# A new order of the work in a gated state-space layer, with stores issued by GpSimd and other rows for the state

## The chip, the cores and the metric

The kernel runs on one core of a Trainium2 chip. The metric is the device time of one execution in microseconds, the median of several. A core has four computing engines: PE (TensorE, matrix products), DVE (VectorE), ACT (ScalarE) and POOL (GpSimd). SP (SyncE) only issues DMAs here. Every engine takes its own instructions strictly in order and waits on semaphores for the others. The 16 DMA engines of the core carry out what the issuing queues give them.

## The reference

The input is `x`, 8 sequences of 1024 tokens with 512 channels, in float32. Two residual layers follow one another.

The first is an attention layer with 16 heads whose projections are modulated by a condition vector. The change does not touch it.

The second is a gated state-space layer. For every token it computes, cut to what matters:

```
xr, gate = split(x @ W_in.T);  xr += t_emb
xc = silu(causal_conv4(xr) + b_conv)
xn = layernorm(xc)
Bm, Cm, dt = split(xn @ W_xproj.T)          # 16 values each
Ad = 1 - tanh(A_log) * 0.01 * tanh(dt @ W_dt.T + b_dt)
Bd = Bm * min(norm(xn), 1)
h  = clip(h * Ad[:, None] + Bd[:, None] * xn[None, :], -10, 10)     # h: 16 x 1024 per sequence
y  = Cm @ h + D * xn
out = x + (y * silu(gate)) @ W_out.T
```

The recurrence over `h` has 1024 steps, one for each token, and each needs the one before.

## The kernel before

The state of a step has 16 rows for each of 8 sequences, 128 rows in all, one on each SBUF partition, and 1024 columns. The recurrence is rescaled by the running product of the decays, so that a step is one addition with limits on VectorE (`step`, L802): `h = limit(h + xb)`. `xb` is the normalised token `xn`, copied to the 16 rows of its sequence and multiplied by a weight for each row. The copying is done by DMA: `spill` (L622) writes 16 tokens of all sequences (512 KB) from SBUF to DRAM, and `fetch` (L765) reads them back for four steps at a time with 8 broadcasts, one for each sequence, of 256 KB each: 16 rows of 16 KB. `rows(b)` (L514) says which partitions a sequence has: partitions 0 to 63 hold sequences 0 to 3, 64 to 127 hold 4 to 7, and a sequence's 16 rows lie 4 apart. `xb` has three buffers of four steps.

ACT multiplies the weights in (`weigh`, L779), two steps ahead. After four steps `products` (L784) sums the 16 rows of each sequence with the output weights on PE, 16 matrix passes in all. `h` has six buffers, so a step waits until the products of the step six before it are done.

Everything else in the layer is done by chunks of 32 tokens, which are two tiles of 16. For one chunk the work runs like this: `load_x1` reads the layer's input; `conv_mm` (8 blocks) multiplies it by `W_in` on PE; `conv_in` copies it and starts the convolution on ACT; `conv_taps` adds three taps on DVE; `conv_out` applies silu on ACT. `flip_mm` transposes on PE; `stats`, `center`, `deviation` and `scale` make the layer norm on DVE, with a square root on ACT. `spill` follows. `squares` and `lengths` make the norm. `skip` multiplies the tile by `D` in place, so it must wait until the spill has read it. `p_mm`, `p_out`, `p_flip`, `params`, `params_mm` and `params_out` make the 48 parameters of each token; `spread` (L665) sends them to the state's rows with 8 small DMAs (`bca`); `decay` and `weights` make the scan's weights from them. Later `order` and `gate_mm` compute the gate, `add_y` and `gate_y` join it to `y`, `out_flip`, `out_copy` and `out_mm` project it, and `out_store` and `out_send` store it with four DMAs a tile.

The order is written by hand. A plan gives each piece a step (`at(n, f, ...)`), counted from `p0`, one chunk before the chunk's own steps begin; `n0 = p0 + 32` is its first own step. The program is emitted step by step: first `h` of the step, then the pieces planned for it. So three chunks are at work in one stretch of 32 steps, and the plan decides the order of instructions on every engine. A step of the plan is no time: an engine goes on as soon as its semaphores allow. All DMAs of the layer are issued by SP, in the plan's order; each waits for the eighth before it of the same kind of queue, and a broadcast of a new group waits for its `xb` buffer.

Of the kernel before, what the change touches and what calls it, by code (L numbers as in the profile page):

```python
# [15 lines left out]
P = 128  # L16
B = 8
# [6 lines left out]
NS = 16  # L24
TC = 32
TT = 16
EPS = 1e-5
EPS_DM = 1e-8


@with_exitstack
def modulated_attention(ctx, tc, const, x1_d, xu_d, S, x, xT, cond, wT, ident, sT):
# [80 lines left out]
    with tc.tile_pool(name="w0", bufs=2) as wp:  # L113
        s2T = wp.tile([P, 2 * KH, B], F32, name="s2T")
        nc.scalar.activation(s2T, sT, AF.Square)
        for n, name in enumerate(NAMES):
# [5 lines left out]
            for o in range(KH):  # L122
                for k in range(KH):
# [6 lines left out]
                    )  # L130
            nc.vector.tensor_scalar_add(dc[:, n], d_ps, EPS_DM)
        nc.scalar.activation(dc, dc, AF.Sqrt)
# [266 lines left out]
def gated_scan(ctx, tc, const, x1_d, S, w_in, w_conv, cols, ln_g, ln_b, w_x, w_xd, w_dt, b_dt, a_log,  # L399
# [10 lines left out]
    nc = tc.nc  # L410
    NCH = S // TC
    CW = B * TC
    NT = TC // TT
# [18 lines left out]

    def load_chunk(c):
        x1 = two.tile([P, KH, B, TC], F32, name="x1")
        nc.sync.dma_start(
            out=x1.rearrange("p k b t -> p k (b t)"),
            in_=x1_d[c].rearrange("(k p) b t -> p k (b t)", p=P),
        )
        return x1

    win_sb = wp.tile([P, KH, 2 * DI], F32, name="win")
    nc.sync.dma_start(out=win_sb[:, :, 0:DI], in_=w_in[:, 0:DI].rearrange("(k p) o -> p k o", p=P))
    x1_now = load_chunk(0)
    cw = load(w_conv.rearrange("(k p) j -> p k j", p=P), "cw", [P, KI, 4])
    cb = load(cols["b_conv"], "cb", [P, KI])
# [18 lines left out]
    xp = few[0:NS, 0 : 3 * CW].rearrange("p (n b t) -> p n b t", n=3, b=B)  # L464
# [48 lines left out]

    def rows(b):  # L514

        r0 = 64 * (b // 4) + b % 4
        return slice(r0, r0 + 4 * (NS - 1) + 1, 4)

    def by_rows(ap):

# [10 lines left out]
    def at(n, f, *args):  # L531
        plan.setdefault(n, []).append(lambda: f(*args))
# [4 lines left out]
    def load_x1(st, c):  # L537
        st["x1"] = load_chunk(c)
# [82 lines left out]

    def spill(st, i):  # L622
        st["xd", i] = dr.tile([32, 4, DI], F32, tag="xd", name="xd")
        nc.sync.dma_start(out=st["xd", i].rearrange("n r c -> r n c"), in_=st["xt", i])

    def squares(st, i):
        if i == 0:
# [37 lines left out]
    def spread(st):  # L665
        st["bca"] = one.tile([P, 3, TC], F32, name="bca")
        for b in range(B):
            nc.sync.dma_start(out=st["bca"][rows(b)], in_=xp[:, :, b, :])

    def decay(st):  # L670
        bd, cm, ad = (st["bca"][:, n] for n in range(3))
# [83 lines left out]
    def out_send(st, c, i):  # L755
        o_sb = st.pop("o_sb")
        t0 = c * TC + i * TT
        for r in range(4):
            dst = out[:, t0 : t0 + TT, :].rearrange("b (q r) o -> r q b o", r=4)[r]
            nc.sync.dma_start(out=dst, in_=o_sb[32 * r : 32 * r + 32, :])  # L760

    xbs = {}
    hs = {}
# [1 line left out]
    def fetch(g):  # L765

        c, t = divmod(4 * g, TC)
        i, q = divmod(t // 4, TT // 4)
        xb = xbp.tile([P, 4, DI], F32, name="xb")
        for b in (0, 4, 1, 5, 2, 6, 3, 7):  # L770
            src = sts[c]["xd", i].rearrange("(q b) r c -> q b (r c)", q=4)[q, b]
            nc.sync.dma_start(  # L772
                out=xb[rows(b)].rearrange("p r c -> p (r c)"),
                in_=src.unsqueeze(0).to_broadcast([NS, 4 * DI]),
            )
        for r in range(4):
            xbs[4 * g + r] = xb[:, r]
# [35 lines left out]
    for c in range(NCH):  # L813
        st, n0 = sts[c], c * TC
        p0 = n0 - TC
        if c > 0:
            at(p0 - 14, load_x1, st, c)
        at(p0 - 9, begin, st)
        for k in range(KI):
            at(p0 - 8 + 2 * k, conv_mm, st, k)  # L820
            at(p0 - 7 + 2 * k, conv_in, st, k)
            at(p0 - 5 + 2 * k, conv_taps, st, k, (0, 1))
            at(p0 - 4 + 2 * k, conv_taps, st, k, (2,))
            at(p0 - 3 + 2 * k, conv_out, st, k)
        for i in range(NT):
            f0 = p0 + 13 + 4 * i
            at(f0, flip_mm, st, i, 0)
            at(f0, flip_mm, st, i, 1)
            at(f0 + 1, stats, st, i, 0)
            at(f0 + 1, stats, st, i, 1)  # L830
            at(f0 + 1, center, st, i)
            at(f0 + 2, deviation, st, i)
            at(f0 + 3, scale, st, i)
            at(f0 + 4, spill, st, i)
            at(f0 + 4, squares, st, i)
            at(p0 + (20, 26)[i], skip, st, i)
        at(p0 + 14, p_mm, st)
        at(p0 + 16, p_out, st)
        at(p0 + 17, p_flip, st)
        at(p0 + 21, lengths, st)  # L840
        for i in range(NT):
            at(p0 + 22 + i, params, st, i)
            at(p0 + 25 + i, params_mm, st, i)
            at(p0 + 26 + i, params_out, st, i)
        at(p0 + 27, spread, st)
        at(p0 + 30, decay, st)
        at(p0 + 31, weights, st, 0)
        at(n0 + 4, weights, st, 1)

        for i, (xo, gm, gs, ey) in enumerate(  # L850
            ((-2, (1, 5), (3, 7), (21, 22, 25, 28)), (17, (22, 23), (24, 25), (38, 39, 41, 45)))
        ):
            at(n0 + xo, order, st, i)
            at(n0 + ey[0], add_y, st, i)
            at(n0 + ey[1], gate_y, st, i)
            for half in range(2):
                at(n0 + gm[half], gate_mm, st, i, half)
                at(n0 + gs[half], gate, st, i, half)
                at(n0 + ey[2] + half, out_flip, st, i, half)
                at(n0 + ey[2] + 1 + half, out_copy, st, i, half)  # L860
                at(n0 + ey[3] + 2 * half, out_mm, st, i, half)
            at(n0 + ey[3] + 4, out_store, st, i)
            at(n0 + ey[3] + 6, out_send, st, c, i)
    for g in range(S // 4):
        at(4 * g - 9, fetch, g)
        at(4 * g + 4, products, g)
# [13 lines left out]
@with_exitstack  # L880
def network(ctx: ExitStack, tc: tile.TileContext, S, ins, out):
    nc = tc.nc
    const = ctx.enter_context(tc.tile_pool(name="const", bufs=1))
    dram = ctx.enter_context(tc.tile_pool(name="dram", bufs=1, space=DRAM))
    x1_d = dram.tile([S // TC, H, B, TC], F32, name="x1_d")
    xu_d = dram.tile([2, H, S], F32, name="xu_d")
    ident = const.tile([P, P], F32, name="ident")
    nc.sync.dma_start(out=ident, in_=ins["ident"])
    sT = const.tile([P, 2 * KH, B], F32, name="sT")
    nc.sync.dma_start(out=sT, in_=ins["condT"].rearrange("(k p) b -> p k b", p=P))  # L890
    with tc.manual_schedule():
# [74 lines left out]
```

## Time and profile before

| | |
|---|---|
| runs, median (lowest to highest) | 6274.84 us (6273.12 to 6277.6) |
| the profiled execution, its span | 6262.97 us, 6261.2 us |
| PE busy over the span | 93% |
| DVE busy | 72% |
| ACT busy | 61% |
| POOL busy (first layer only) | 20% |
| DMA queue of SP, share of 16 engines | 45.4% |
| first and last `h` start | 3557.8 and 6240.3 us |

A line of the timelines gives the start and the length in microseconds, the engine, the line of the kernel, the operation with its output and inputs, how many instructions were merged, and in brackets the idle time before them with what ended it. A line of waits gives the waiting engine and operation, whom it waited for, the sum in microseconds, the number of times, and the longest. Lines with SPq are DMA issues on SP's queue.

The second layer begins after some 3470 us; the profile's 40 slices show GpSimd idle in all of it.

### The profile page before, as it was taken

How to read it: one execution, taken by the hardware profiler on the slowest of the kernel's cores; microseconds unless marked ns; L12 is line 12 of the kernel's file. 1: busy time of each engine (PE TensorE's matmuls, PEld its weight loads, DVE VectorE, ACT ScalarE, POOL GpSimd, SP SyncE). 2: the span in 40 equal slices, each digit the busy share in tenths (PEclk: the TensorE clock that was granted, in tenths of full speed). 3: DMA queues.
4: the chain of work that ended last, by engine and by line, in shares of the span. 5: the costliest groups of instructions: out<-in, count | busy, mean ns of one | idle time of the engine just before them, and what ended most of it. 6: DMA issues, size and time to landing. Idle time of an engine off the chain costs nothing.

```text
span 6261.2 us, 112973 instructions
## 1 busy us (share of the span) xinstructions
PE 5796.5 (93%) x42960; PEld 3314.5 (53%) x42960; DVE 4484.0 (72%) x6917; ACT 3843.8 (61%) x6743; POOL 1266.2 (20%) x1156
## 2 busy tenths in 40 slices
PE   7999999999999999999999699999999999999998
PEld 5555555655555555555555444444444444444443
DVE  2666666656667666666665488888888888888887
ACT  3555655655556556555554477777777777677675
POOL 2433433434334334343332000000000000000000
PEclk8999999999999999999999899999999999999999
DMA  2112111112121111121211678888888888888787
GB/s 70 35 30 71 30 55 49 35 48 67 30 70 31 55 48 35 48 67 30 55 28 55 177 224 223 221 221 228 225 223 227 222 222 228 220 224 226 221 223 198
DMA packets 396859, 781.65 MB, mean 125 GB/s; under 512 B 196496, under 2 KB 295056, under 8 KB 363552
## 3 DMA queue, kind: packets, MB, share of 16 engines
q1 hardware_dynamic: 396320, 774.44, 45.4%
q8 instruction: 341, 5.59, 0.4%
q14 instruction: 198, 1.62, 0.1%
HBM read 663.62 MB, written 83.89 MB: 119 GB/s over the span
## 4 chain that ended last, share of the span: by engine, by line
PE 60%; DMA 14%; DVE 10%; ACT 8%; SPq 5%; issue 3%; POOL 0%; DVEq 0%; ACTq 0%; POOLq 0%
PE mm_ps L153 16%; PE t_ps L262 13%; PE s_ps L252 9%; DMA xb<-xd 8%; PE mm_ps L269 8%; DVE h L806 5%; DMA xd<-xt 4%; PE o_ps L745 4%; SPq L772 4%; PE in_ps L547 4%; ACT pr L370 3%; PE y_ps L793 3%; ACT pT L367 1%; PE g_ps L705 1%; PE in_ps L551 1%
## 5 line engine op out<-in xcount | busy, mean ns | idle before, releaser
L360 DVE TENSOR_REDUCE nmax<-s_ps 128x1 f32<-128x1024 f32 x1024 | 1206.2, 1220 | 478.0 <-PE s_ps L255 477.4
L806 DVE CUSTOM_DVE_ANT_0 h<-h,xb,lim 128x1024 f32<-128x1024 f32 x1024 | 1374.7, 1342 | 209.7 <-PE y_ps L793 71.7
L367 ACT COPY pT<-t_ps 128x512 f32<-128x512 f32 x1024 | 549.8, 589 | 1378.8 <-PE t_ps L262 1378.5
L262 PEld LDWEIGHTS t_ps<-ident,pr 128*128 128x128 f32 x8192 | 909.7, 141 | 646.4 <-issue 453.2
L782 ACT ACTIVATE xb<-xb,ws 128x1024 f32<-128x1024 f32 x1024 | 1135.9, 1145 | 62.4 <-DVE ws L682 31.3
L370 ACT ACTIVATE pr<-s_ps,nmax 128x1024 f32<-128x1024 f32 x1024 | 1139.6, 1127 | 6.1 <-DVE nmax L360 5.7
L262 PE MATMUL t_ps<-ident,pr 128*128 128x128 f32 x8192 | 1096.1, 277 | 30.7 <-ACT pT L367 28.5
L793 PE MATMUL y_ps<-h,yw 128*32 128x512 f32 x4096 | 675.5, 617 | 159.7 <-DVE h L806 159.6
L252 PE MATMUL s_ps<-kT,qT 32*128 32x512 f32 x2048 | 601.1, 641 | 4.4 <-ACT pr L370 4.4
L389 POOL TENSOR_SCALAR pr<-pr,rinv 128x1024 f32<-128x1024 f32 x512 | 572.6, 1118 | 145.6 <-DVE rinv L388 142.9
L255 PE MATMUL s_ps<-k,q 32*128 32x512 f32 x2048 | 578.2, 640 | 0.0
L269 PEld LDWEIGHTS mm_ps<-pT,vt 128*32 128x32 f32 x16384 | 438.0, 110 | 235.1 <-issue 94.3
L705 PE MATMUL g_ps<-win,x1t 128*128 128x512 f32 x1024 | 508.5, 643 | 58.1 <-ACT sq_ps L631 51.3
L269 PE MATMUL mm_ps<-pT,vt 128*32 128x128 f32 x16384 | 517.6, 274 | 47.5 <-ACT vt L200 18.5
L547 PE MATMUL in_ps<-x,win 128*128 128x256 f32 x2048 | 490.9, 383 | 28.9 <-ACT xt L733 17.4
L375 POOL TENSOR_SCALAR pr<-pr,rinv 128x1024 f32<-128x1024 f32 x256 | 286.5, 1119 | 1109.5 <-PE t_ps L262 741.0
L547 PEld LDWEIGHTS in_ps<-x,win 128*128 128x128 f32 x2048 | 389.8, 192 | 152.4 <-issue 71.6
L384 POOL TENSOR_SCALAR pr<-pr,rinv 128x1024 f32<-128x1024 f32 x256 | 286.3, 1118 | 882.6 <-DVE rinv L383 855.8
L745 PE MATMUL o_ps<-wout,xt 128*128 128x512 f32 x1024 | 463.7, 596 | 0.7 <-ACT xt L733 0.7
L793 PEld LDWEIGHTS y_ps<-h,yw 128*32 128x32 f32 x4096 | 133.9, 110 | 545.6 <-DVE h L806 295.0
L381 DVE COPY pT<-t_ps 128x512 f32<-128x512 f32 x512 | 352.2, 688 | 77.2 <-PE t_ps L262 76.8
L705 PEld LDWEIGHTS g_ps<-win,x1t 128*128 128x128 f32 x1024 | 198.2, 204 | 384.6 <-issue 229.5
(129 smaller groups left out, 6750.7 us busy)
## 6 DMA issues: line engine op xcount, KB each, us to landing
xb<-xd SPq DMA_DIRECT2D x2048, 256.0 KB
xd<-xt SPq DMA_DIRECT2D x64, 512.0 KB
xq<-in_x SPq DMA_DIRECT2D x16, 1024.0 KB
q<-qT SPq DMA_DIRECT2D x128, 128.0 KB
xr<-in_xT SPq DMA_DIRECT2D x64, 256.0 KB
xu_d<-xr SPq DMA_DIRECT2D x64, 256.0 KB
xr<-xu_d SPq DMA_DIRECT2D x64, 256.0 KB
x_d<-xr SPq DMA_DIRECT2D x64, 256.0 KB
```

The source lines that it names most:

```text
L153: nc.tensor.matmul(ps, w, x, start=(k == 0), stop=(k == KH - 1))
L252: nc.tensor.matmul(s_ps[i][:, 0:HW], st["q"][r, qc], st["k"][r, 0:HW], start=True, stop=True)
L262: nc.tensor.transpose(ps[:, j], pr[:, c0 : c0 + P], ident)
L269: nc.tensor.matmul(av[r], vt[:, kt, r], pT[:, i, kt], start=(kt == 0), stop=(kt == KT - 1), skip_group_check=True,)
L360: nc.vector.tensor_reduce(nmax[i], s_ps[i], AX.X, ALU.max, negate=True)
L370: nc.scalar.activation(fresh[i], s_ps[i], AF.Exp, bias=nmax[i], accum_out=rsum[i])
L547: nc.tensor.matmul(ps, win_sb[:, kk, k * P : (k + 1) * P], st["x1"][:, kk].rearrange("p b t -> p (b t)"), start=(kk == 0), stop=False,)
L705: nc.tensor.matmul(ps, st["xo", i][:, k], win_sb[:, k, DI + half * 512 : DI + (half + 1) * 512], start=(k == 0), stop=(k == KH - 1),)
L745: nc.tensor.matmul(ps, st["gT", i][:, k, :], wout_sb[:, k, :], start=False, stop=(k == KI - 1), skip_group_check=True,)
L782: nc.scalar.mul(xbs[n], xbs[n], sts[c]["ws"][:, t : t + 1])
L793: nc.tensor.matmul(st["y", i][32 * r : 32 * r + 32, hf * 512 : (hf + 1) * 512], yws[i][:, 4 * q + r, :], hs[4 * g + r][:, hf * 512 : (hf + ...
L806: nc.vector._custom_dve(dve_ops.TENSOR_ADD_SAT, out=h, in0=last["h"], in1=xbs.pop(n), s0=lim[:, 0, t : t + 1], s1=lim[:, 1, t : t + 1],)
```

## The change

Three things change. First, the plan: nearly every piece of a chunk gets another step. Second, `load_chunk`, `spill`, `spread` and `out_send` issue their DMAs from GpSimd; the broadcasts of `fetch` stay on SP. Third, a sequence's rows: sequences 0 to 3 have rows 32 to 95, 4 apart, so each has 8 rows in either half of the partitions; 4 and 5 have rows 0 to 31, 6 and 7 rows 96 to 127, 2 apart. The order of the eight broadcasts changes with it, and the host builds its small tables (`mask_y`, `b_dt`, `a_log`) by the same map. What is computed, and the number of instructions that compute it, stay.

```diff
+def state_rows(b):
+    if b < B // 2:
+        return 32 + b, 4
+    return 96 * (b // 6) + b % 2, 2
...
     def load_chunk(c):
         x1 = two.tile([P, KH, B, TC], F32, name="x1")
-        nc.sync.dma_start(
+        nc.gpsimd.dma_start(
...
     def rows(b):
-        r0 = 64 * (b // 4) + b % 4
-        return slice(r0, r0 + 4 * (NS - 1) + 1, 4)
+        r0, d = state_rows(b)
+        return slice(r0, r0 + d * (NS - 1) + 1, d)
...
     def spill(st, i):
-        nc.sync.dma_start(out=st["xd", i].rearrange("n r c -> r n c"), in_=st["xt", i])
+        nc.gpsimd.dma_start(out=st["xd", i].rearrange("n r c -> r n c"), in_=st["xt", i])
...
     def spread(st):
         for b in range(B):
-            nc.sync.dma_start(out=st["bca"][rows(b)], in_=xp[:, :, b, :])
+            nc.gpsimd.dma_start(out=st["bca"][rows(b)], in_=xp[:, :, b, :])
...
     def out_send(st, c, i):
-            nc.sync.dma_start(out=dst, in_=o_sb[32 * r : 32 * r + 32, :])
+            nc.gpsimd.dma_start(out=dst, in_=o_sb[32 * r : 32 * r + 32, :])
...
-        for b in (0, 4, 1, 5, 2, 6, 3, 7):
+        for b in (4, 6, 0, 1, 5, 7, 2, 3):
```

The plan's steps, counted from `p0`; where two are given they are for the two tiles, and with a stroke for the two halves of a tile:

```
                before                            after
load_x1         -14                               -11
begin           -9                                -14
conv_mm k       -8+2k                             -9+2k
conv_in k       -7+2k                             -8+2k
conv_taps k     -5+2k, -4+2k                      -7+2k, -6+2k
conv_out k      -3+2k                             -5+2k
flip_mm         13, 17                            10, 13
stats, center   14, 18                            11, 15
deviation       15, 19                            12, 16
scale           16, 20                            14, 17
spill           17, 21                            15, 21
squares         17, 21                            17, 19
skip            20, 26                            30, 22
p_mm, p_out, p_flip   14, 16, 17                  16, 19, 20
lengths         21                                19
params          22, 23                            21, 20
params_mm       25, 26                            22, 21
params_out      26, 27                            24, 24
spread, decay   27, 30                            26, 30
weights         31, 36                            35, 34
order           30, 49                            36, 49
gate_mm         33/37, 54/55                      39/42, 50/53
gate            35/39, 56/57                      41/43, 52/58
add_y, gate_y   53 54, 70 71                      53 56, 65 67
out_flip        57/58, 73/74                      58/58, 71/72
out_copy        58/59, 74/75                      60/65, 75/75
out_mm          60/62, 77/79                      61/67, 77/78
out_store       64, 81                            68, 81
out_send        66, 83                            73, 83
```

`fetch`, `products` and `weigh` keep their steps: 9 before a group's first step, 4 after it, and 2 before each step.

More of the change, by code (lines that the diff above doesn't have):

```diff
@@ L816, in gated_scan @@
         if c > 0:
-            at(p0 - 14, load_x1, st, c)
-        at(p0 - 9, begin, st)
+            at(p0 + -11, load_x1, st, c)
+        at(p0 + -14, begin, st)
         for k in range(KI):
[L820 to L845, printed above, removed]
-        at(p0 + 30, decay, st)
[L847 to L863, printed above, removed]
+            at(p0 + -9 + 2 * k, conv_mm, st, k)
@@ new lines, in gated_scan @@
+            at(p0 + -8 + 2 * k, conv_in, st, k)
+            at(p0 + -7 + 2 * k, conv_taps, st, k, (0, 1))
+            at(p0 + -6 + 2 * k, conv_taps, st, k, (2,))
+            at(p0 + -5 + 2 * k, conv_out, st, k)
+        at(p0 + 10, flip_mm, st, 0, 0)
+        at(p0 + 10, flip_mm, st, 0, 1)
+        at(p0 + 11, stats, st, 0, 0)
+        at(p0 + 11, stats, st, 0, 1)
+        at(p0 + 11, center, st, 0)
+        at(p0 + 12, deviation, st, 0)
+        at(p0 + 14, scale, st, 0)
+        at(p0 + 15, spill, st, 0)
@@ new lines, in gated_scan @@
+        at(p0 + 17, squares, st, 0)
+        at(p0 + 30, skip, st, 0)
+        at(p0 + 13, flip_mm, st, 1, 0)
+        at(p0 + 13, flip_mm, st, 1, 1)
+        at(p0 + 15, stats, st, 1, 0)
+        at(p0 + 15, stats, st, 1, 1)
+        at(p0 + 15, center, st, 1)
+        at(p0 + 16, deviation, st, 1)
+        at(p0 + 17, scale, st, 1)
+        at(p0 + 21, spill, st, 1)
+        at(p0 + 19, squares, st, 1)
+        at(p0 + 22, skip, st, 1)
+        at(p0 + 16, p_mm, st)
+        at(p0 + 19, p_out, st)
@@ new lines, in gated_scan @@
+        at(p0 + 20, p_flip, st)
+        at(p0 + 19, lengths, st)
+        at(p0 + 21, params, st, 0)
+        at(p0 + 22, params_mm, st, 0)
+        at(p0 + 24, params_out, st, 0)
+        at(p0 + 20, params, st, 1)
+        at(p0 + 21, params_mm, st, 1)
+        at(p0 + 24, params_out, st, 1)
+        at(p0 + 26, spread, st)
+        at(p0 + 30, decay, st)
+        at(p0 + 35, weights, st, 0)
+        at(p0 + 34, weights, st, 1)
+        at(p0 + 36, order, st, 0)
+        at(p0 + 39, gate_mm, st, 0, 0)
@@ new lines, in gated_scan @@
+        at(p0 + 41, gate, st, 0, 0)
+        at(p0 + 42, gate_mm, st, 0, 1)
+        at(p0 + 43, gate, st, 0, 1)
+        at(p0 + 53, add_y, st, 0)
+        at(p0 + 56, gate_y, st, 0)
+        at(p0 + 58, out_flip, st, 0, 0)
+        at(p0 + 60, out_copy, st, 0, 0)
+        at(p0 + 61, out_mm, st, 0, 0)
+        at(p0 + 58, out_flip, st, 0, 1)
+        at(p0 + 65, out_copy, st, 0, 1)
+        at(p0 + 67, out_mm, st, 0, 1)
+        at(p0 + 68, out_store, st, 0)
+        at(p0 + 73, out_send, st, c, 0)
@@ new lines, in gated_scan @@
+        at(p0 + 49, order, st, 1)
+        at(p0 + 50, gate_mm, st, 1, 0)
+        at(p0 + 52, gate, st, 1, 0)
+        at(p0 + 53, gate_mm, st, 1, 1)
+        at(p0 + 58, gate, st, 1, 1)
+        at(p0 + 65, add_y, st, 1)
+        at(p0 + 67, gate_y, st, 1)
+        at(p0 + 71, out_flip, st, 1, 0)
+        at(p0 + 75, out_copy, st, 1, 0)
+        at(p0 + 77, out_mm, st, 1, 0)
+        at(p0 + 72, out_flip, st, 1, 1)
+        at(p0 + 75, out_copy, st, 1, 1)
+        at(p0 + 78, out_mm, st, 1, 1)
@@ L864, in gated_scan @@
+        at(p0 + 81, out_store, st, 1)
+        at(p0 + 83, out_send, st, c, 1)
     for g in range(S // 4):
@@ L913, in cols @@
         return np.asarray(v).reshape(-1, P).T
-    mask_y = np.broadcast_to(
-        np.eye(B, dtype=np.float32).reshape(2, 1, 4, B), (2, NS, 4, B)
-    ).reshape(P, B)
+    batch_of, state_of = np.zeros(P, int), np.zeros(P, int)
+    for b in range(B):
+        r0, d = state_rows(b)
+        batch_of[r0 + d * np.arange(NS)] = b
+        state_of[r0 + d * np.arange(NS)] = np.arange(NS)
+    mask_y = np.eye(B, dtype=np.float32)[batch_of]
     cond_k = np.zeros((P, P), np.float32)
@@ L923, in rows @@
     def rows(v):
-        return np.tile(np.repeat(np.asarray(v), 4), 2)[:, None]
+        return np.asarray(v)[state_of][:, None]
     arrays = {
```

## The prediction

> **What bounds the kernel now.** I read the table by stage first, then the waits and timelines of one chunk, then the scan's last chunk. The second layer is a recurrence of 1024 steps, 32 to a chunk. In the timeline of VectorE, step `h` runs from 3557.8 to 6241.6 us, so the layer's steady part is 2683.8 us, 31.65 chunks of 84.8 us. The table by stage (columns PE, weight loads, DVE, ACT, POOL busy; PE clock; DMA share; GB/s):
>
> ```profile
> 4700.00:5100.00 400.00, 364.31 (x1614) 190.71 (x1614) 335.36 (x483) 285.33 (x492) 0.00 (x0) 0.98 0.81 224
> ```
>
> PE looks 91% busy, DVE 84%, DMA 81%, ACT 71%. Nobody is full; GpSimd does nothing. The PE figure flatters: the products `y_ps` stand busy while they wait for `h`. Timeline of TensorE in one chunk:
>
> ```profile
> 4614.96 1.38 PE L793 MATMUL y_ps<-h,yw 128*32 128x512 f32 x6
> 4619.45 3.14 PE L793 MATMUL y_ps<-h,yw 128*32 128x512 f32 x10 [3.10 <-DVE h L806]
> ...
> 4647.67 1.92 PE L793 MATMUL y_ps<-h,yw 128*32 128x512 f32 x16
> 4649.52 3.70 PE L745 MATMUL o_ps<-wout,xt 128*128 128x512 f32 x8
> 4653.06 1.89 PE L547 MATMUL in_ps<-x,win 128*128 128x256 f32 x8
> 4654.79 0.60 PE L551 MATMUL in_ps<-ident,cond 128*128 128x256 f32 x2
> 4655.22 1.89 PE L547 MATMUL in_ps<-x,win 128*128 128x256 f32 x8
> ```
>
> Undisturbed (start to start) one group's products take 1.85, half an output projection 3.54, one convolution block 2.16. With such prices PE has 70 us of work in 84.8. The waits of 4300 to 5500 us (14.15 chunks) say who stops whom:
>
> ```profile
> PE y_ps L793 <- DVE h L806: 67.7, 42, 3.1
> DVE xt L637 <- DMA xd<-xt: 58.8, 28, 4.1
> DVE h L806 <- PE y_ps L793: 36.6, 15, 3.7
> DVE stat L597 <- PE x_ps L592: 32.8, 14, 2.4
> ```
>
> PE waits for DVE and DVE for PE in the same chunk: `h` has six buffers, so products and steps can part by about one group of four steps. A group with much PE work stops DVE, the next with much DVE work stops PE. On top, DVE waits 4.2 us a chunk in `skip` for the spill to land. That is the bound: an uneven plan, not a full engine.
>
> The DMA is close behind. First the start of the layer, where little else moves. Timeline of VectorE:
>
> ```profile
> 3533.03 1.22 DVE L637 TENSOR_TENSOR xt<-xt,d_bc 128x1024 f32<-128x1024 f32 x1 [7.09 <-DMA xd<-xt]
> ```
>
> The spill that it waited for, on the SP queue:
>
> ```profile
> 3522.58 0.65 SPq L624 DMA_DIRECT2D xd<-xt  x1
> ```
>
> The chain of waits in the last chunk:
>
> ```profile
> 6198.04 6.98 DMA xb<-xd
> 6205.02 0.02 issue
> 6205.03 7.35 DMA xb<-xd
> 6212.38 0.02 issue
> 6212.40 7.02 DMA xb<-xd
> ```
>
> A spill of 512 KB takes 10.4 us with no broadcast in flight. Eight broadcasts (2.1 MB) take about 7.3 us when DMA alone paces the steps: 0.91 us each, 18 GB/s on each of 16 engines.
>
> [...] Against their being the bound now: DVE waits for broadcasts only some 2 us a chunk, and SP waits 129 us in these 14 chunks for DVE to free a slot.
>
> [...]
>
> **The change, part by part.** No arithmetic is added. 19 of 83 DMA issues per chunk (2 spills, 8 output stores, 8 `bca`, 1 `x1`) leave SP for GpSimd; 64 broadcasts stay.
>
> (1) Plan. I lay each line's price on its step, before and after, and add per group of four steps. Prices (us): PE products 1.87, gate half 3.54, output half 3.44 (+0.9 residual in the first), convolution block 2.16, `p_mm` 3.46, flips 0.3 to 0.5. DVE `h` 1.26, tap 0.47, stats 0.65, center 1.57, scale 1.20, skip, add and gate 1.15, params 0.80, decay 1.48, weights 0.41, deviation 0.42. ACT weigh 1.05, conv_in 0.73, conv_out 0.67, order 1.28, squares 1.25, params_out 0.70, gate, copies and store 0.5. A group lasts as long as its fullest engine:
>
> Before: PE 9.7, 9.7, 2.9, 14.0, 3.1, 9.0, 8.0, 14.0; DVE 7.9, 10.6, 6.9, 8.3, 9.5, 11.6, 7.1, 9.8; ACT at most 9.0 (group 7). Maxima 9.7+10.6+6.9+14.0+9.5+11.6+9.0+14.0 = 85.3.
>
> After: PE 9.6, 8.1, 6.8, 10.6, 8.9, 8.7, 7.2, 10.5; DVE 11.0, 7.9, 8.4, 9.5, 7.0, 8.9, 8.5, 10.5; ACT 8.8 and 9.3 in groups 2 and 5. Maxima 11.0+8.8+8.4+10.6+9.3+8.9+8.5+10.5 = 76.0.
>
> Totals are the same in both (PE 70.3, DVE 71.7, ACT 57.4). DVE's 71.7 of 84.8 is the 84% of the table by stage. The sum of maxima for before lies 0.5 us from the measured 84.8: what it leaves out (spill waits, slots) is about what the slack across groups gives back. I take 76.0 for after, with less to smooth and less to wait for.
>
> (2) Spill and skip. First tile: skip moves from 3 steps after the spill to 15; its share of the 4.2 us goes. Second tile: the plan puts skip one step after the spill, but GpSimd can issue it once scale (5 steps before skip) and the older output store ahead of it are done. From scale DVE has five `h`, lengths, two params and add_y, 9.4 us, before skip. At today's 10.4 us plus 1 to 2 us of queue, DVE stops 2 to 3 us; spread over 16 engines, none. I take 1.0 on top of 76.0: 77.0 us per chunk, range 74 to 80.
>
> (3) SP queue. The 19 issues at about 0.6 us leave it; also the wait for every eighth DMA before, which after a spill held the broadcasts. SP then holds 64 x 0.63 = 40 us of issues in 77. It was not the bound: nothing by itself, cover for DMA.
>
> (4) `bca` from GpSimd. It is issued after params_out (step 24), wanted by decay (step 30): six steps of 2.4 us, 14.4. The trace shows no GpSimd DMA. From below I bound an issue by SP's 0.63 us[...]. At 1 us[...] eight issues and 2 us of landing take 10: hidden. At 2 us: 18, so 3.6 us a chunk late; ACT stops in tanh, behind it weigh and then `h`.
>
> (5) Row map. Broadcasts need 64 x 0.91 = 58 us a chunk; with stores spread evenly (128 KB per engine, 7 us) 65, below 77. Worth nothing on the path if so[...].
>
> (6) Ends. At the start the first skip no longer holds the second tile's scale (7.1 us idle at 3533), nor a spill the `bca` issues: -8. The last store from GpSimd: +2.
>
> Sum on the profiled execution (6262.97, span 6261.2): -7.8 x 31.65 = -247, -8, +2 = -253, 6010; the median of the runs is 12 higher: 6022.
>
> **Rivals.** DMA becomes the bound: GpSimd's stores still sit on four engines together[...]. Then 1440 KB at 18 GB/s is about 82 us a chunk: -2.8 x 31.65 = -89, with the ends 6180[...]
>
> Floor: slack across groups swallows the rest and DVE alone counts, 71.7 plus 1 us of gaps between back-to-back `h` (0.17 each): 72.7, -383, 5890. Against: single waits between engines stay.
>
> Slower: the `bca` issues are slow. Six steps cover eight issues up to (14.4 - 2)/8 = 1.55 us; the 7.8 us gained are gone at 2.5 us each. At 3 us they come 24 + 2 - 14.4 = 11.6 us late, 3.8 more than gained: +120 and the ends, 6390.[...]
>
> That the row map does nothing visible is part of the first case.
>
> **How the numbers follow.** Even plan, 74 to 80 us a chunk (5930 to 6120): 0.60. DMA-bound, 6120 to 6260: 0.18. Floor, below 5930: 0.07. Slower: 0.12. Within 0.2% (12 us, about what a measurement of this kernel can tell): 0.03. Range 5925 to 6235 leaves out the slower case, most of the floor and a little of the DMA case.
>
> **What would show it.** Right: a chunk of about 77 us, DVE near 93%, no long `y_ps` wait for `h` and no stats wait over 1 us, the first tile's skip without a wait, first `h` near 3550. DMA rival: `h` or ACT's weigh wait for `xb`, SP never waits for DVE. Slower: ACT waits for `bca` in the tanh of decay (L672 before the change). My number is wrong if single waits inside a group, which the sum of maxima cannot see, grow past what slack gives back.

## The result, and the profile after

| | before | after |
|---|---|---|
| runs, median (lowest to highest) | 6276.22 us (6273.12 to 6281.06) | 6315.93 us (6313.14 to 6327.47) |
| ratio, with its 95% interval | | 1.0072 [1.006, 1.0083] |
| span of the profiled execution | 6261.2 us | 6325.4 us |
| first and last `h` start | 3557.8 and 6240.3 us | 3562.3 and 6298.7 us |
| end of the span after the last `h` start | 20.9 us | 26.7 us |

The change makes the kernel 0.7% slower. The forecast was 6022 us and faster; 6316 lies outside its range too. The profiled executions lie 64.2 us apart, the medians 39.7, so the profiled one of after is a little above its median. Of the 64.2, 4.5 us lie ahead of the first `h`, 53.9 in the recurrence and 5.8 behind it. A chunk should have become 77.0 us long; it became 86.5 on average (2736.4 us over 31.65 chunks).

The table by stage of the kernel after. The columns are as before: length of the stage, then PE, weight loads, DVE, ACT and POOL busy, TensorE's granted clock, DMA share, GB/s. The first line is one steady stretch, the others are parts of one chunk.

```profile
4700.00:5100.00 400.00, 335.46 (x1577) 183.75 (x1575) 328.67 (x466) 281.04 (x483) 54.34 (x94) 0.92 0.82 222
...
4630.00:4652.00 22.00, 22.00 (x95) 11.07 (x94) 20.95 (x29) 17.50 (x30) 4.52 (x7) 1.00 0.88 227
4653.00:4667.00 14.00, 0.76 (x7) 0.52 (x5) 7.07 (x6) 3.60 (x8) 3.57 (x7) 0.64 0.98 232
4667.00:4690.00 23.00, 21.55 (x100) 13.83 (x101) 14.40 (x24) 11.69 (x21) 0.51 (x1) 0.85 0.61 163
```

The mean over 400 us (DVE 82%, DMA 82%) looks like the kernel before. The parts do not. For 22 us of a chunk PE is always busy and DVE nearly so, which is what an even plan should look like. Then, for 14 us, PE does nothing and DVE is busy half of the time, while the DMA engines are busy 98% of the time. And in the 23 us after that PE runs at 0.85 of its clock. The waits of 4300 to 5500 us (14 chunks) of the kernel after name the two places:

```profile
PE in_ps L554 <- DMA x<-x_d: 184.5, 14, 14.7
DVE xt L644 <- DMA xd<-xt: 139.0, 14, 11.9
ACT xb L789 <- DMA xb<-xd: 79.2, 24, 7.4
ACT rs L621 <- DVE mv L609: 49.3, 14, 4.2
DVE xc L574 <- ACT xc L567: 40.1, 26, 6.9
```

PE waits 13.2 us a chunk for `x1` (the DMA `x<-x_d`), once each time. DVE waits 9.9 us a chunk in `skip` for the spill, and 2.9 for the convolution that stands behind PE's wait. The three waits that bound the kernel before are no longer among the long ones: in the whole layer `y_ps` waits only 15.9 us for `h`, where it was 67.7 in 14 chunks. So the plan did even out the work, and two landings took the place of what it removed.

One chunk on TensorE, kernel after (timeline):

```profile
4652.94 0.82 PE L663 MATMUL xp_ps<-ident,pt 128*128 128x128 f32 x6
4668.45 3.75 PE L554 MATMUL in_ps<-x,win 128*128 128x256 f32 x8 [14.69 <-DMA x<-x_d]
4671.99 1.06 PE L558 MATMUL in_ps<-ident,cond 128*128 128x256 f32 x2
4672.98 2.45 PE L800 MATMUL y_ps<-h,yw 128*32 128x512 f32 x16
4675.36 1.99 PE L554 MATMUL in_ps<-x,win 128*128 128x256 f32 x8
```

And what GpSimd issued for it, from its timeline:

```profile
4636.14 0.69 POOL L631 DMA_DIRECT2D xd<-xt  x1 [21.09 <-DVE xt L627]
4640.68 2.35 POOL L767 DMA_DIRECT2D out<-o_sb  x4 [3.85 <-ACT o_sb L759]
4644.32 0.69 POOL L631 DMA_DIRECT2D xd<-xt  x1 [1.29 <-DVE xt L627]
4645.00 0.80 POOL L442 DMA_DIRECT2D x<-x_d  x1
4662.39 3.57 POOL L675 DMA_DIRECT2D bca<-few  x7 [16.59 <-ACT few L668]
```

The two spills, four output stores and `x1` are issued within 10 us of each other: the two spills 8.2 us apart, `x1` 0.7 us after the second. In the kernel before the spills are 15.4 us apart. There SP issued them and `x1`:

```profile
4613.90 0.57 SPq L624 DMA_DIRECT2D xd<-xt  x1
4614.59 0.40 SPq L435 DMA_DIRECT2D x<-x_d  x1
...
4629.30 0.57 SPq L624 DMA_DIRECT2D xd<-xt  x1
```

They landed 10.5 and 11.3 us later, by the end of `skip`'s waits (kernel before, VectorE):

```profile
4624.37 1.22 DVE L637 TENSOR_TENSOR xt<-xt,d_bc 128x1024 f32<-128x1024 f32 x1 [3.12 <-DMA xd<-xt]
...
4640.62 1.23 DVE L637 TENSOR_TENSOR xt<-xt,d_bc 128x1024 f32<-128x1024 f32 x1 [1.39 <-DMA xd<-xt]
```

In the kernel after `skip` of the second tile waits longer (VectorE):

```profile
4660.66 1.23 DVE L644 TENSOR_TENSOR xt<-xt,d_bc 128x1024 f32<-128x1024 f32 x1 [6.71 <-DMA xd<-xt]
```

The second spill lands at 4660.66, 16.3 us after its issue, and `x1` at 4668.45, 23.4 us after its own. For the spill this chunk is a mild one: from 4300 to 5500 us the second spill of a chunk lands 20.0 us after its issue, the first 14.5 (medians). DVE stopped from 4653.95 on, PE from 4653.76 on. The convolution block that comes first after PE's idle time takes 3.75 us, the next 1.99. The granted clock is at 0.50 from 4657.03 to 4674.10, that is also for the first 5.65 us of PE's work, and at 1.00 from there to 4690.

### The profile page after: what moved, and what is told of

Read it like the earlier page. It is cut to its first block, busy times and chain, and to the rows that moved or that the text cites. A ratio compares the mean times of both kernels' runs of the same rounds, so it can differ in the third digit from the quotient of the medians.

```text
span 6325.4 us, 113455 instructions
## 1 busy us (share of the span) xinstructions
PE 5664.1 (90%) x42960; PEld 3322.2 (53%) x42960; DVE 4474.7 (71%) x6917; ACT 3837.2 (61%) x6743; POOL 1617.6 (26%) x1764
## 5 line engine op out<-in xcount | busy, mean ns | idle before, releaser
L554 PE MATMUL in_ps<-x,win 128*128 128x256 f32 x2048 | 551.9, 417 | 411.9 <-DMA x<-x_d 411.9
L554 PEld LDWEIGHTS in_ps<-x,win 128*128 128x128 f32 x2048 | 411.8, 208 | 578.9 <-issue 460.9
L800 PE MATMUL y_ps<-h,yw 128*32 128x512 f32 x4096 | 515.3, 611 | 23.6 <-DVE h L813 15.9
L712 PE MATMUL g_ps<-win,x1t 128*128 128x512 f32 x1024 | 470.9, 603 | 2.5 <-ACT x1t L707 2.5
L574 DVE SCALAR_TENSOR_TENSOR xc<-xr,cw,xc 128x256 f32<-128x256 f32 x768 | 369.2, 481 | 111.9 <-ACT xc L567 98.6
L767 POOL DMA_DIRECT2D out<-o_sb x256 | 151.2, 597 | 1148.7 <-ACT o_sb L759 1144.4
L388 DVE COPY pT<-t_ps 128x512 f32<-128x512 f32 x512 | 351.7, 687 | 79.2 <-PE t_ps L269 78.8
```

The source lines that it names most:

```text
L554: nc.tensor.matmul(ps, win_sb[:, kk, k * P : (k + 1) * P], st["x1"][:, kk].rearrange("p b t -> p (b t)"), start=(kk == 0), stop=False,)
L800: nc.tensor.matmul(st["y", i][32 * r : 32 * r + 32, hf * 512 : (hf + 1) * 512], yws[i][:, 4 * q + r, :], hs[4 * g + r][:, hf * 512 : (hf + ...
```

## The experiments

Ratios are to the kernel before on the same chip. What an expectation calls one part "alone" is that part put into the kernel before; all else is the kernel after with the edit shown.

### Which part costs?

**rows_only**: the row map and the order of the broadcasts, on the kernel before.

```diff
-        for b in (0, 4, 1, 5, 2, 6, 3, 7):
+        for b in (4, 6, 0, 1, 5, 7, 2, 3):
...
+        r0, d = state_rows(b)
+        return slice(r0, r0 + d * (NS - 1) + 1, d)
```

> The kernel before with the new state rows and the new order of broadcasts alone. Theory A (GpSimd's large transfers land late because they take turns with the broadcasts; the plan is good): broadcasts get about 13% slower, as the last chunk of the changed kernel shows (8.3 us for eight against 7.4 before), but stay hidden behind the steps: 6270 to 6300, with the loss in the last chunk, where DMA alone paces the steps (+6 us). Theory C (the rows make DMA the bound): a chunk of 84.8 becomes 89 us, 6380 to 6420. If the rows help as the prediction had it, the last chunk's groups take under 7.3 us.

**pool_only**: the four `nc.sync` that became `nc.gpsimd` (`x1`, spill, `bca`, output), on the kernel before.

```diff
-        nc.sync.dma_start(out=st["xd", i].rearrange("n r c -> r n c"), in_=st["xt", i])
+        nc.gpsimd.dma_start(out=st["xd", i].rearrange("n r c -> r n c"), in_=st["xt", i])
```

> The kernel before with its four kinds of small DMA and stores issued by GpSimd alone, old plan, old rows. Theory A: x1 lands some 21 us after its issue where the plan gives 16, and each spill 16 us where the plan gives 8, so PE and DVE stop for 5 and about 2 x 6 us a chunk more than now's 4.2: 6450 to 6700. Theory B (the new plan is too tight, whoever issues): no change, 6250 to 6300.

**plan_only**: the new steps alone; all DMAs on SP, rows as before.

```diff
-            at(p0 - 14, load_x1, st, c)
+            at(p0 + -11, load_x1, st, c)
...
-            at(p0 - 8 + 2 * k, conv_mm, st, k)
+            at(p0 + -9 + 2 * k, conv_mm, st, k)
```

> The kernel before with the new plan alone, all DMAs on SP, old rows. Theory A: the balance of the groups shows; x1 and the second spill are held up behind the broadcasts on SP, but land in 8 to 11 us: 6030 to 6280, a chunk of 77 to 84 us. Theory B: 6290 or more, PE waiting for x1 10 us or more a chunk here too.

**x1_sp**: the kernel after, with `x1` loaded from SP again.

```diff
-        nc.gpsimd.dma_start(
+        nc.sync.dma_start(
             out=x1.rearrange("p k b t -> p k (b t)"),
```

> The changed kernel with the load of x1 alone back on SP. Theory A: PE's wait for x1 falls from 13.2 us a chunk to 5 to 8, the wait for the second spill stays at about 10: 6316 less 31 x 5 to 8, 6070 to 6160. Theory B: the load issued two steps before its use stays late: 6290 or more.

| | median us | ratio |
|---|---|---|
| rows_only | 6285.63 | 1.0031 [1.0016, 1.0045] |
| pool_only | 6370.04 | 1.0157 [1.0142, 1.0172] |
| plan_only | 6361.68 | 1.0145 [1.013, 1.0161] |
| x1_sp | 6326.76 | 1.009 [1.0075, 1.0105] |

Each part alone makes the kernel slower, and the three together cost less than the plan alone or GpSimd alone. With the plan alone, the waits are those of the kernel after (kernel plan_only, waits of 4300 to 5500 us):

```profile
PE in_ps L547 <- DMA x<-x_d: 205.8, 14, 15.6
DVE xt L637 <- DMA xd<-xt: 182.0, 14, 13.8
```

So the two stops come with the plan, on either queue. On SP the reason is in part another: in one chunk the second spill leaves at 4662.06, 10.9 us after `scale`, behind broadcasts and stores, and lands 12.2 us later. GpSimd alone keeps the old waits between products and steps and gets new ones for `bca` (kernel pool_only, same view):

```profile
PE y_ps L793 <- DVE h L806: 75.6, 58, 3.1
DVE xt L637 <- DMA xd<-xt: 68.8, 14, 7.9
ACT bca L672 <- DMA bca<-few: 49.8, 13, 4.8
...
DVE bca L673 <- ACT bca L672: 39.7, 14, 3.8
```

With `x1` on SP it lands 8.6 us after its issue in place of 21.2 (medians), but it is issued later, behind a group's broadcasts, and PE waits as long as before: 191.3 us in 14 chunks. Moving `x1` alone to the other queue mends nothing.

### Is it the wait in skip, or the shape of x1's load?

Two thoughts were tried here: that `x1` lands late because it is cut into rows of 1 KB, and that DVE's stop in `skip` is the loss, so that a later `skip` would mend it.

**packed**: `x1` laid out in DRAM so that its load reads rows of 4 KB.

```diff
-    x1_d = dram.tile([S // TC, H, B, TC], F32, name="x1_d")
+    x1_d = dram.tile([S // TC, P, KH, B, TC], F32, name="x1_d")
```

> The changed kernel with x1 kept in DRAM in the order of the partitions, so that a row of the load is 4 KB instead of four times 1 KB; nothing else. Theory A (each packet from GpSimd's queue waits for a broadcast's packet, so the count of packets sets the landing): x1 lands in 8 to 11 us instead of 21, PE's wait for it falls from 13 us a chunk to 0 to 3; the wait for the second spill (10 us) stays and then sets the chunk at 80 to 85: 6080 to 6210. Theory D (the bytes set the landing, or the load waits behind the spill on its queue): it still lands in 17 to 21 us, 6290 to 6330.

**skip_late**: `skip` of the second tile seven steps later.

```diff
-        at(p0 + 22, skip, st, 1)
+        at(p0 + 29, skip, st, 1)
```

> The changed kernel with skip of the second tile seven steps later (29 instead of 22). The two waits lie beside each other in time: while DVE waits for the spill, PE waits for x1. So theory A expects DVE's wait for the spill to go and the time to stay within 6280 to 6320, since x1 alone still stops PE, and through h's buffers DVE. If the spill is the one that decides: 6050 to 6150.

**packed_late**: both.

> Both edits, the packed x1 and the later skip. Theory A: both waits go and the sum of the groups' maxima comes out, 76 to 78 us a chunk: 5950 to 6040. Theory E (with the waits gone the DMA is the next bound): 80 to 84 us a chunk, ACT waiting for broadcasts more than 3 us a chunk: 6080 to 6200.

**packed_late_oldrows**: both, with the rows and the order of the broadcasts of the kernel before.

> Both edits and the old rows with the old order of the broadcasts. If the new rows cost broadcasts: 10 to 60 us faster than the one with both edits and new rows. If they help, as the prediction had it: slower by 10 to 100 us. If the steps cover the broadcasts either way: within 10 us.

| | median us | ratio |
|---|---|---|
| packed | 6314.33 | 1.0073 [1.0056, 1.009] |
| skip_late | 6476.02 | 1.0329 [1.0314, 1.0344] |
| packed_late | 6475.36 | 1.0326 [1.031, 1.0341] |
| packed_late_oldrows | 6362.85 | 1.0148 [1.0133, 1.0163] |

The first thought fell: with rows of 4 KB `x1` lands 21.7 us after its issue and nothing moves. The second fell harder. With `skip` out of the way the kernel lost another 160 us (kernel skip_late, waits of 4300 to 5500 us):

```profile
PE in_ps L554 <- DMA x<-x_d: 229.2, 13, 21.4
DVE xc L574 <- ACT xc L567: 189.8, 13, 19.8
```

I read the stop in `skip` as a relief for the DMA engines: while DVE stands, no `xb` buffer comes free, and SP must hold the next broadcasts back; without it they go on. That is not shown by itself: SP waits 378.6 us for `h` in this stretch of skip_late, as it does in the kernel after (380.2). What is shown is that `x1` lands 25.7 us after its issue in place of 21.2 (medians) and PE waits 17.6 us a chunk. The second spills land no later as a rule (19.5 us against 20.0, medians), though some do: one issued at 4708.16 lets the `bca` issue that waits for it go at 4736.11, 28.0 us later. So the stop in `skip` was not the loss. What was left to try was the time that the spill spends on the DMA engines.

### The spill, in one piece or in four

The destination of a spill begins with a dimension of 4, the four quarters of a token's rows in DRAM. That it runs on 4 engines for this reason was the author's assumption; no run had shown it. The theory, called F where a letter is used: these 512 KB on few engines, beside broadcasts that keep the engines busy (16 of their packets are under way at once for 636 of the 1200 us from 4300 to 5500 us of the kernel before), are what lands late, and `x1` stands behind them on the same engines. The same bytes as four DMAs, one for each quarter, each begin with a dimension of 32 on both sides. If F holds, they spread and land sooner.

**split**: the kernel after with the spill cut in four. **before_split** is the same cut in the kernel before, on SP.

```diff
-        nc.gpsimd.dma_start(out=st["xd", i].rearrange("n r c -> r n c"), in_=st["xt", i])
+        for r in range(4):
+            nc.gpsimd.dma_start(out=st["xd", i][:, r], in_=st["xt", i][32 * r : 32 * r + 32])
```

> The changed kernel with each spill cut into four DMAs of 32 partitions by 1024, so that the slowest dimension of both sides is 32 instead of 128 and 4[...]. The packed load left x1's landing at 21.7 us, so the count of packets is not the reason. Theory F (the spill runs on four engines, which are full; the load of x1 stands behind it on them): the spill lands in 5 to 8 us instead of 16, x1 in 6 to 10, both waits go: 5970 to 6060, a chunk of 76 to 79 us. Theory G (a transfer from GpSimd gets a small share of every engine while broadcasts are in flight, however it is cut): the spill still takes over 12 us, x1 over 17: 6250 to 6330.

> The kernel before with each spill cut into four DMAs. Theory F: DVE's wait for the spill (4.2 us a chunk, 130 us in all) goes, part of it taken up by other waits: 6140 to 6230; the spill lands in about 5 us. If the landing does not depend on the shape: 6265 to 6300, a little slower for six more issues a chunk.

**split_late** has the cut and `skip` at 29; **split_late_oldrows** is that on the old rows.

> The same with skip of the second tile at 29. Theory F: the spill is in time already, so within 20 us of the one before. Theory G: 6400 to 6480, as with the uncut spill.

> The same again with the old rows and the old order of broadcasts. With the uncut spill the new rows cost 113 us. If they cost broadcasts on all engines and broadcasts set the pace again: 40 to 120 us faster than with the new rows. If with the spill cut the steps cover the broadcasts: within 20 us.

| | median us | ratio |
|---|---|---|
| split | 6099.32 | 0.9724 [0.971, 0.9739] |
| before_split | 6166.4 | 0.9829 [0.9815, 0.9844] |
| split_late | 6119.8 | 0.9762 [0.9747, 0.9776] |
| split_late_oldrows | 6114.99 | 0.9746 [0.973, 0.9762] |

One line of the program is worth 217 us in the kernel after and 105 in the kernel before. The landings of 4300 to 5500 us of the kernel after (columns: DMA, queue and operation, number, size, median us from issue to landing):

```profile
xd<-xt POOLq DMA_DIRECT2D x27, 512.0 KB, 16.3
...
x<-x_d POOLq DMA_DIRECT2D x13, 512.0 KB, 21.2
```

The same view of split:

```profile
xd<-xt POOLq DMA_DIRECT2D x123, 128.0 KB, 4.9
...
x<-x_d POOLq DMA_DIRECT2D x15, 512.0 KB, 10.8
```

A piece of the spill lands in 4.9 us (the four are issued within 2.0 us) in place of 16.3 for the whole, and `x1`, which was not touched, in half its time. Late `skip` now costs 20 us where it had cost 160.

The traces also keep a record of every packet that the DMA engines moved, with its queue, size, start and length. It shows four at a time. In pool_only the last spill, issued at 6243.3, has GpSimd's queue to itself: of its 128 packets of 4 KB four are under way for 5.9 us, five for 0.3, and otherwise fewer. In split the four pieces issued at 4627.31 have 14 packets or more under way for 1.5 us. From GpSimd the four are not always the same: in x1_sp its queue carries only spills, output stores and the small `bca`, and from 4300 to 5500 us seven to twelve packets of 4 KB are under way for 25 us. On SP, in the kernel before, the packets of spills and output stores together are mostly four at a time and hardly ever more than five.

The record shows too who stands behind whom. In the kernel before, `x1` comes in 512 packets of 1 KB. Of the load that SP issued at 4614.59, right behind a spill, 384 packets had ended 5.8 us later; the other 128, a quarter, ended from 8.5 to 10.6 us after the issue, and the spill's last packet in between, at 9.3. All 31 loads behind a spill show such a gap behind the 384th packet, of 1.7 to 3.7 us. In before_split the gap is gone, and the 512 packets are over 4.9 us after the issue (median) in place of 10.8. I read this as a spill on four of the sixteen engines, with `x1` behind it on these four and only there; the record does not name the engines. What it shows is that on SP's queue a quarter of `x1` ends with the spill and the rest does not. From GpSimd the packets of both have 4 KB and can't be told apart; that `x1` stands behind the spill there too is read from the landings (21.2 us behind whole spills, 10.8 behind cut ones).

What is left in split (waits of 4300 to 5500 us, 15 chunks):

```profile
PE in_ps L554 <- DMA x<-x_d: 96.6, 15, 9.1
DVE xc L574 <- ACT xc L567: 87.7, 30, 7.8
...
DVE xt L645 <- DMA xd<-xt: 4.7, 1, 4.7
```

The wait in `skip` is gone (one in 15 chunks), but PE still stops 6.4 us a chunk for `x1`. That is the part of the change that the prediction's sum does not contain at all: `load_x1` moved from 6 steps ahead of the first `conv_mm` to 2.

### What the plan and GpSimd earn once the spill is cut

**plan_split** and **pool_split** are plan_only and pool_only with the cut spill.

> The kernel before with the new plan and each spill cut in four; all DMAs stay on SP, old rows, x1 at 11 steps before p0. Theory A (the plan earns the gain, GpSimd only serves it by keeping spill and x1 out of SP's queue of broadcasts): x1 is issued late behind a group's broadcasts, TensorE waits 8 to 14 us a chunk for it, 6150 to 6250 us. Theory B (with the spill cut the queue does not matter): 6090 to 6120 us, as the changed kernel with the cut spill.

> The kernel before with its four kinds of DMAs issued by GpSimd and each spill cut in four; old plan, old rows. Theory A (the plan earns the gain): about the kernel before with the cut spill, 6150 to 6190 us, with the waits between products and steps as there. Theory B (leaving SP earns part of it): 6100 to 6140 us. If bca stays late as with the queues alone and an uncut spill, 6200 us or more.

| spill cut in four | DMAs on SP | on GpSimd |
|---|---|---|
| old plan | 6166.4, 0.9829 [0.9815, 0.9844] (before_split) | 6175.15, 0.9846 [0.9831, 0.986] (pool_split) |
| new plan | 6159.33, 0.9817 [0.9801, 0.9834] (plan_split) | 6099.32, 0.9724 [0.971, 0.9739] (split, new rows) |

Neither earns anything alone; the intervals of the first three overlap. With the new plan on SP the landings are late (kernel plan_split, same waits):

```profile
PE in_ps L547 <- DMA x<-x_d: 123.3, 15, 9.0
DVE xt L638 <- DMA xd<-xt: 99.2, 15, 7.3
```

and with GpSimd under the old plan the uneven groups are still there (kernel pool_split, same waits):

```profile
PE y_ps L794 <- DVE h L807: 74.4, 49, 3.1
...
DVE h L807 <- PE y_ps L794: 45.3, 15, 3.6
DVE stat L597 <- PE x_ps L592: 35.1, 15, 2.4
```

The plan removes the waits between the engines and asks for prompt landings; a queue of its own makes the landings prompt. On this evidence each is worth something only with the other, 60 to 76 us together. How much of that the rows give is not separated, since of the four kernels split alone has the new ones. But split_late_oldrows, on the old rows and with the later `skip`, still lies 44 us below plan_split.

### x1 earlier, and a spill that isn't kept waiting

**split_early**: the cut, and `x1` four steps earlier, the earliest step at which its buffer is free. **split_early_oldrows** is that on the old rows.

```diff
-            at(p0 + -11, load_x1, st, c)
+            at(p0 + -15, load_x1, st, c)
```

> The changed kernel with each spill cut in four, and the load of x1 four steps earlier (15 before p0 in place of 11), the earliest at which its buffer is free. Theory A (the rest of the miss is x1's late load): TensorE's wait for x falls from 6.4 us a chunk to 0 to 2, VectorE's wait for the convolution behind it goes, a chunk is 76 to 77 us, the time 6010 to 6050 us. Theory B (single waits inside the groups, or the DMA as a whole, hold the chunk at 78 to 80 us anyway): the wait for x goes, others grow, 6080 to 6110 us.

> The same on the old rows. If the rows cost only when the DMA paces the steps: within 15 us of split_early. If the new rows slow the broadcasts wherever they run: 20 us or more below it.

**split_early_out**: besides, the second tile's output stores three steps later, so that GpSimd issues them behind the spill; in **split_early_out_skip** the second tile's `skip` is two steps later too.

```diff
-        at(p0 + 83, out_send, st, c, 1)
+        at(p0 + 86, out_send, st, c, 1)
...
-        at(p0 + 22, skip, st, 1)
+        at(p0 + 24, skip, st, 1)
```

> The changed kernel with the spill cut, x1 four steps earlier, and the second tile's output stores three steps later (86 in place of 83), so that GpSimd issues them behind the spill. If the spill's late issue makes skip wait: the spill is issued 3.8 us earlier, skip waits under 1 us, PE's wait of 3.9 us for h behind it goes, and a chunk is 74 to 76 us: 5930 to 6010 us. If the landing is slow in itself: skip still waits 3 to 4 us, 6030 to 6060 us.

> The same with skip of the second tile two steps later (24 in place of 22). If the order of the issues was all: within 15 us of the kernel with the stores moved. If the landing is slow in itself: 30 us or more below it, with no wait in skip. If skip then falls into the group that is already full and delays what follows: 10 to 30 us above it.

| | median us (lowest to highest) | ratio |
|---|---|---|
| split_early | 6047.53 (6027.4 to 6053.18) | 0.9634 [0.9615, 0.9653] |
| split_early_oldrows | 6081.23 (6075.91 to 6087.79) | 0.9694 [0.9679, 0.9708] |
| split_early_out | 5959.0 (5931.24 to 5972.05) | 0.9497 [0.9469, 0.9526] |
| split_early_out_skip | 5975.49 (5953.42 to 5999.56) | 0.9542 [0.9519, 0.9565] |

With `x1` earlier PE's wait for it goes, and 52 us with it; the next thing is late. Kernel split_early, timeline of VectorE:

```profile
4694.20 1.22 DVE L645 TENSOR_TENSOR xt<-xt,d_bc 128x1024 f32<-128x1024 f32 x1 [4.36 <-DMA xd<-xt]
```

Timeline of GpSimd in the same kernel:

```profile
4677.86 0.80 POOL L442 DMA_DIRECT2D x<-x_d  x1 [3.82 <-ACT x1t L708]
4678.65 0.64 POOL L768 DMA_DIRECT2D out<-o_sb  x1
4681.88 1.76 POOL L768 DMA_DIRECT2D out<-o_sb  x3 [2.59 <-issue]
4683.64 1.51 POOL L632 DMA_DIRECT2D xd<-xt  x3
4686.40 0.49 POOL L632 DMA_DIRECT2D xd<-xt  x1 [1.25 <-DMA x<-x_d]
```

`scale` was done at 4679.9, but the spill left at 4683.64, behind four stores that stand ahead of it in GpSimd's program, and its last piece at 4686.40, after `x1` had landed: that is the wait for the eighth DMA before it on GpSimd's queue. (In the kernel after, no issue of GpSimd starts before the eighth ahead of it has landed, in 600 of 600 cases; the closest comes 0.28 us behind the landing.) With the stores behind the spill, kernel split_early_out, GpSimd's timeline shows the whole spill leave at once:

```profile
4706.62 0.82 POOL L442 DMA_DIRECT2D x<-x_d  x1 [3.83 <-ACT x1t L708]
4708.98 1.95 POOL L632 DMA_DIRECT2D xd<-xt  x4 [1.54 <-DVE xt L627]
4710.92 1.83 POOL L768 DMA_DIRECT2D out<-o_sb  x3
```

Its table by stage (columns as before):

```profile
4700.00:5100.00 400.00, 396.78 (x1888) 218.07 (x1887) 386.02 (x550) 331.63 (x572) 79.43 (x146) 1.00 0.94 262
```

And three of its `gate_y` on VectorE, one for each chunk (the other tile's, in between, are left out):

```profile
5112.81 1.22 DVE L730 TENSOR_TENSOR gate<-xt,gate 128x1024 f32<-128x1024 f32 x1
...
5186.02 1.22 DVE L730 TENSOR_TENSOR gate<-xt,gate 128x1024 f32<-128x1024 f32 x1
...
5258.78 1.22 DVE L730 TENSOR_TENSOR gate<-xt,gate 128x1024 f32<-128x1024 f32 x1
```

In this execution, which with 5931 us is the fastest of the four, these chunks are 73.2 and 72.8 us long, DVE is busy 97% of the stretch above, and PE's granted clock is 1.00 there. This kernel, 5959 us, is faster than both that were given: 0.9497 [0.9469, 0.9526]. `skip` two steps later gives no more: it is 16 us slower, with intervals that just overlap. And in split_early_out `skip` waits 7.3 us for the spill from 4300 to 5500 us, where split_early had 64.1. So the order of the issues was the reason, not a landing that is slow in itself.

## Why the prediction was wrong

**Step (1), the plan: right.** The sum of the fullest engine's work in each group gave 76.0 us. The kernel after spends 22 of its 88 us in a stretch with PE at 100% and DVE at 95%, the waits for `y_ps`, `h` and `stats` went, and split_early_out, whose landings are in time, does a chunk in 74.3 by the measure that gives 86.5 above (2350.4 us over 31.65 chunks). That execution is 28 us, 0.9 us a chunk, faster than the median. So the chunk lies between the 76.0 and the 72.7 of the Floor rival: the slack across groups takes a little more than the sum leaves out.

**Step (2), spill and skip: the wrong size, 1.0 us taken, 9.9 measured.** Its two inputs were a 10.4 us landing and 9.4 us of cover. The cover was read well: GpSimd issued the spill without delay at 4644.32, and DVE ran out of other work 9.6 us later, at 4653.95. The landing was that of a spill from SP at the start of the layer, with only `x1`'s load near it; here two spills leave GpSimd 8.2 us apart and the second takes 16.3, or 20.0 in the median chunk, 10.4 more than the cover of 9.6. The plan moved them together in time: the two `scale` went from 4 steps apart to 3, and the first tile's `skip`, which stood between them and waited, is later now. The step did not look at that. The 1.0 us stands between a stop of 2 to 3 us and none, should the spill spread over 16 engines; that it might do so from GpSimd was the author's assumption, and it is not borne out: its packets go four at a time, and it is as slow from GpSimd alone (11.5 us, pool_only) as from SP (10.5 and 11.3). In x1_sp GpSimd's transfers together have up to twelve packets under way, so they don't all share the same four engines, but a spill still lands only 17.1 us after its issue (median).

**The step that is missing: `load_x1`.** The table of steps shows it going from 14 to 11 before `p0`, and `conv_mm` from 8 to 9, so 6 steps of cover became 2. No line of the sum priced it. It is the longest stop: PE waits 13.2 us a chunk, and the convolution taps behind it stop DVE for 2.9. In the kernel before `x1` was issued 16.6 us ahead of its first use (4614.59 to 4631.20) and its packets took 10.6, so its landing needed no look; in the kernel after PE wanted it 8.8 us after its issue. This stop and that of step (2) fall at the same time, so the two waits don't add up to the loss, which is 9.5 us a chunk (86.5 against 77.0); in the experiments the cut spill is worth 217 us and the earlier `x1` 52 more. Then comes what PE loses beyond the idle time. PE is idle from 4653.76 to 4668.45, and the granted clock is at 0.50 from 4657.03 to 4674.10: the first convolution block took 3.75 us against 1.89, and the 5.65 us that PE worked at half clock cost it some 2.8 us (an estimate: half of the 5.65).

**Step (3), SP's queue "nothing by itself": right for the old plan** (pool_split against before_split: +9 us, within the intervals), **wrong for the new one**, which needs its spill and `x1` not to stand behind broadcasts (plan_split against split: 60 us, with the new rows in it).

**Step (4), `bca`: right in the kernel after.** An issue takes 0.51 us on GpSimd (seven in 3.57), a store 0.6, a spill 0.69, and nobody waits for `bca`. The 2 us of landing that the step counts with agrees with the start of the layer in the kernel before, where the last `bca` issue starts at 3552.40 and ACT, waiting for it, goes on at 3554.32; in the kernel after the median is 5.0. So the rival "Slower", which held the only loss in the forecast, had the wrong mechanism. Under the old plan, three steps from `spread` to `decay`, `bca` from GpSimd is late by 3.6 us of ACT a chunk (pool_only).

**Step (5), the row map: not nothing, and not of one sign.** New rows against old: +14 us alone; +113 where landings pace the steps (packed_late against its old rows); 5 in split_late, within the intervals; and -34 in split_early, where the landings are about 1 us shorter on the new rows (medians: broadcasts 5.5 us against 6.2, `x1` 7.7 against 8.9). What decides the sign stays open: no run shows how a transfer depends on the rows, and the order of the eight broadcasts, which changed with them, was not taken apart.

**Step (6), the ends:** -8 and +2 were said, +4.5 and +5.8 came. At the start one wait of 7.1 us went, and `skip` got another of 9.5, with 7.4 in the convolution behind it.

**The rival "DMA becomes the bound"** had half of the mechanism that the runs bear out: stores that go four packets at a time, beside broadcasts. But it had them all on the same four engines, full without a pause, 1440 KB at 18 GB/s in 82 us a chunk. That was an estimate on the author's assumption: a sixteenth of the 64 broadcasts and of `x1`, a quarter of the spills and of the output stores. From GpSimd the transfers don't all share four (x1_sp, seven to twelve packets under way for 25 us), and in truth the DMA engines pause (61% in the 23 us after a stop, with little but broadcasts to move), because DVE and PE stop for two landings one after the other and then have no work to cover with. Of the rival's signs one came, ACT's wait for `xb` (79.2 us in 14 chunks), and one did not: SP still waits for DVE, 380.2 us in the same stretch. Which engines a spill takes is not in the trace. That it goes four packets at a time, and that on SP's queue a quarter of `x1` ends with it, is in the packets; that this is so on GpSimd's queue too is not shown for `x1`.

## What to carry to other kernels

When a plan is moved, list for every DMA the work between its issue and its first use, before and after, and set against it the landing time in the new surroundings (what else is issued within that time, on which queue), not that of a lone transfer. A store like the spill, whose destination begins with a dimension of 4, is worth trying as DMAs that begin with a larger one before anything is planned around it: here the cut into four that begin with 32 was worth 217 us in the kernel after and 105 in the kernel before. Taking away one wait can lengthen another (skip_late lost 160 us so): after each mend look for what is late next, as three edits did here, one after the other, from 6316 to 5959 us.

## What the runs showed of the hardware

- A 512 KB store whose destination's slowest dimension is 4 landed in 10.5 to 11.3 us from SP (before) and in 11.5 (pool_only) or 16.3 (after) from GpSimd, medians; as four stores with a slowest dimension of 32 each piece landed in 4.9 us (split). Packets under way at a time: mostly four for the one (pool_only, 5.9 us), 14 or more for 1.5 us for the other (split). Spills and output stores together have mostly four under way on SP (before: four for 172 us and more than five for 1.8 us, from 4300 to 5500 us), while from GpSimd seven to twelve are under way for 25 us (x1_sp).
- A 512 KB load on SP's queue behind such a store moved 384 of its 512 packets within 3.5 to 7.6 us of its issue and the last 128 only as the store's ended, in the median 10.8 us after it (before, 31 loads); behind cut stores it was over after 4.9 (before_split).
- `x1`'s load, 512 KB as rows of 1 KB or of 4 KB, took 21.2 (after) and 21.7 us (packed) from GpSimd behind uncut spills, 10.8 behind cut ones (split), 7.7 ahead of them (split_early).
- After an idle time of 4.9 us in PE the next convolution block took 3.75 us (split, at 4649.82), as after one of 14.7 us (after, at 4668.45); undisturbed blocks take 1.89 us in both.
- A DMA issue took GpSimd 0.5 to 0.8 us here (after), about SP's 0.4 to 0.7 (before). In these kernels a DMA waits for the eighth before it on its queue, GpSimd's too (after: 600 of 600 issues): in split_early the spill's last piece went at 4686.40, when `x1`, eight issues earlier, had landed.
- Each engine's instructions come in one order throughout: from 3900 to 5900 us of the kernel after the same sequence of 344 on PE, 101 on DVE, 104 on ACT and 19 on GpSimd repeats from chunk to chunk without an exception.
